# The last pass over the edges also norms and turns its rows for the recurrence

## The chip, the cores and the metric

The kernel runs on one core of one Trainium2 chip, in one launch. The metric is the time of an execution on the device in microseconds (us). The engines of the core are PE (matrix products and transposes), DVE (vector operations), ACT (activations and copies), POOL (vector operations and indirect transfers) and SP (it only issues transfers). ACT and POOL issue transfers too.

## The reference: what is computed

There are N = 3125 nodes with rows x of 256 numbers, and 50000 weighted edges, sorted by their target. Four layers follow each other; each adds its result to x:

1. An attention layer over the edges. Each node's normed row gives features for itself and for its neighbours (128 numbers each, in 4 heads of 32); a node sums its neighbours' features with weights from the edges; both halves are normed by head and added to x.
2. A recurrence over the nodes, taken as one sequence of 3125 steps. With xn the layer norm of the new x, a step computes gates from `xn @ U + b` and from the last state through V: `i`, `o` with a sigmoid, `g` with a tanh, `c = h * c + i * g`, `h = o * tanh(c)`. The states h are added to x.
3. Three graph convolutions (256 to 1024, 512 and 256) with norms.
4. A mixture of eight experts.

The change lies where layer 1 ends and layer 2 begins: the row norm

    xn = (x - mean) / sqrt(var + 1e-5)

of every node, and its transpose, which the products with U read.

## The kernel before, in words

The nodes are padded to 25 tiles of 128 rows. Before the last pass, the edges have been scattered into a dense matrix of weights in DRAM, and that matrix is read back in panels. The sum over the neighbours is a matrix product of features and panels. It runs in 9 passes (`passes`, L581) of 7 steps; a pass takes three row tiles of the matrix (the last one takes one) and a step takes a block of 512 columns, that is four node tiles (the seventh block has one). In a step `products` (L505) issues PE's matmuls, and the count transposes (`ct`, L534) with ACT's Sign (L535), whose result goes to DRAM from two buffers `cs` (L536). The sums lie in `agg0`, two halves of 3200 columns in the pool `ep`, and passes 0 to 7 add to them (L544).

In the last pass the products of a block (L518 and L519, 16 for four tiles) read `agg0` itself and leave the sums, centered and turned, in two banks of PSUM. A bank is one of five (`bank`, L409). A generator, `finish` (L546), ends a block in three stages, which the steps of the pass call one step apart:

- A: the attention weights (L555) and the second half (L558) on DVE, and the square on ACT (L560);
- B: the head's variance on DVE (L563, L564), scale (L565) and power -1/2 (L566) on POOL;
- C: norm (L568) and sum into x (L570) on DVE, and the statistics of each new row of x (L573, L574) into `mv_r`.

So step k holds the products of block k, then A of block k, B of block k-1 and C of block k-2. After the pass come the last B and two C (L957), then the variances are copied (L960) and `inv_sqrt_dve` (L131) takes the inverse root of all 25 tiles into `rstd_r`.

What sets the order: the whole phase stands under `manual_schedule` for DVE, PE, ACT and SP. These four keep the order in which the phase's instructions are written. Instructions written after the phase may be placed among them by the scheduler, and POOL's order is the scheduler's too. A tile whose place in memory belonged to earlier tiles waits until they are free.

Then `recurrence_inputs` (L1050) loads V and U in blocks of 128 columns and six columns of biases, all issued by ACT (L1055, L1068, L1070). For each of 25 tiles it norms the row on DVE (`normalize`, L160), transposes its halves on PE into one of two PSUM tiles (L167) and copies them to `xnT` on ACT (L168). The products with U follow, 42 groups (7 stretches of 500 columns, the last of 125, by 6 gate blocks) of two matmuls (L1083), each evicted by ACT into `xg` with its bias (L1085) from one of four PSUM tiles `pu`.

The recurrence itself (L1154 on) is cut into 125 chains that run side by side for 45 + 25 steps; its first instructions are L1158 on PE and L1180 on ACT. While it runs, POOL gathers the lines for the nodes' degrees (L988), and SP moves them (L1009, L1011). `inv_sqrt` (L124) is the form of the inverse root that runs on POOL (L128, L129).

Of the kernel before, what the change touches and what calls it, by code (L numbers as in the profile page):

```python
# [9 lines left out]
F32 = mybir.dt.float32  # L10
# [3 lines left out]
AF = mybir.ActivationFunctionType  # L14
# [78 lines left out]
def kernel(ctx: ExitStack, tc: tile.TileContext, a: dict, out: bass.AP):  # L93
# [300 lines left out]

    weighed, unit_end = [], []
    ec = ctx.enter_context(tc.tile_pool(name="ec", bufs=1))
    extra_i = ec.tile([P, EXTRA], I32, name="extra_i")
    extra_c = ec.tile([P, EXTRA], F32, name="extra_c")
    line_i = ec.tile([P, NT], I32, name="line_i")
# [2 lines left out]
    with ExitStack() as ph:  # L402
# [21 lines left out]
        nc.gpsimd.memset(zeros, 0.0)  # L424


        agg0 = ep.tile([P, 2, NP], F32, name="agg0")
# [77 lines left out]
        def products(q, j, n, t):  # L505
# [40 lines left out]
            def finish():  # L546

                m0, k = j // P, n // P
                g = k * H0
                f = sp.tile([P, CB // P, 4 * DH], F32, name="fa", bufs=3)  # L550
                fh = f[:, :k].rearrange("p n (h k) -> p (n h) k", k=DH)
                for i in range(0, k, 2):
                    h = min(2, k - i)
                    pt = pas[i // 2].rearrange("p (n o d) -> p n o d", n=2, o=2)[:, :h]
                    nc.vector.tensor_tensor(f[:, i : i + h].rearrange("p n (h k) -> p n h k", k=DH),  # L555
                                            pt[:, :, 0, :].rearrange("p n (h k) -> p n h k", k=DH),
                                            att[:, m0 + i : m0 + i + h, :4, None].to_broadcast([P, h, H0, DH]), ALU.mult)
# [5 lines left out]
                nc.vector.tensor_reduce(var[:, :g], sq[:, :k].rearrange("p n (h k) -> p (n h) k", k=DH), AX.X, ALU.add)  # L563
                nc.vector.tensor_scalar(var[:, :g], var[:, :g], 1.0 / DH, 1e-9, op0=ALU.mult, op1=ALU.add)  # L564
                nc.gpsimd.tensor_tensor(f[:, :k], f[:, :k], sc0[:, None, 4 * DH :].to_broadcast([P, k, 4 * DH]), ALU.mult)  # L565
                nc.gpsimd.tensor_tensor(rs[:, :g], var[:, :g], neghalf[:, :g], ALU.pow)  # L566
                yield
                nc.vector.tensor_tensor(fh, fh, rs[:, :g, None].to_broadcast([P, g, DH]), ALU.mult)  # L568
                xs = x[:, m0 : m0 + k, 4 * DH :]
                nc.vector.tensor_add(xs, xs, f[:, :k])  # L570
                for i in range(m0, m0 + k):
                    st = sp.tile([P, 6], F32, name="st")
                    nc.vector.bn_stats(st, x[:, i, :])  # L573
                    nc.vector.bn_aggr(mv_r[:, i, :], st)  # L574
                yield

            if last:
# [3 lines left out]
        def passes(q, k0=0, k1=7):  # L581

            per = len(steps) // len(PASSES)
            for k in range(q * per + k0, q * per + k1):
                while len(panels) <= k + AHEAD and len(panels) < len(steps):
                    panels.append(load(*steps[len(panels)]))
                now = products(*steps[k], panels[k])
                if rest[0] is not None:
                    rest[0]()
                if q == len(PASSES) - 1:  # L590
                    for g in (now, *ending[-2:][::-1]):
                        next(g)
                    ending.append(now)
                    now = None
                rest[0] = now
# [212 lines left out]
        with ExitStack() as eh:  # L808
# [238 lines left out]

    def recurrence_inputs(rp, stats=None):  # L1050

        blocks = [(g, half) for half in range(2) for g in ("i", "o", "c")]
        V = rp.tile([P, 2, 6 * P], F32, name="V")
        for m, (g, half) in enumerate(blocks):
            nc.scalar.dma_start(V[:, :, m * P : (m + 1) * P],  # L1055
                                a["L0_ffn_V_" + g].rearrange("(c p) n -> p c n", p=P)[:, :, half * P : (half + 1) * P])

        xg = rp.tile([P, 6, CH, QW + NB], F32, name="xg")
        nc.vector.memset(xg[:, :, :, :QW], 0.0)
# [2 lines left out]
        with ExitStack() as eh:  # L1062
            up = eh.enter_context(tc.tile_pool(name="u", bufs=1))
            ps = eh.enter_context(tc.tile_pool(name="up", bufs=2, space=PSUM))
            U = up.tile([P, 2, 6 * P], F32, name="U")
            bias = up.tile([P, 6], F32, name="bias")
            for m, (g, half) in enumerate(blocks):
                nc.scalar.dma_start(U[:, :, m * P : (m + 1) * P],  # L1068
                                    a["L0_ffn_U_" + g].rearrange("(c p) n -> p c n", p=P)[:, :, half * P : (half + 1) * P])
                nc.scalar.dma_start(bias[:, m : m + 1],  # L1070
                                    a["L0_ffn_b_" + g][half * P : (half + 1) * P].rearrange("(p o) -> p o", o=1))
            mv, rstd = stats or x_stats(up)
            xnT = up.tile([P, 2, NP], F32, name="xnT")
            for i in range(NT):
                xn = up.tile([P, D], F32, name="xn", bufs=2)
                normalize(xn, i, mv, rstd)
                transposed(ps, xnT[:, :, i * P : (i + 1) * P], xn, 2)
            for b0 in range(0, NB, 20):
                n = min(20, NB - b0)
                for m in range(6):  # L1080
                    pu = ps.tile([P, 20 * CH], F32, name="pu", bufs=4)
                    for c in range(2):
                        nc.tensor.matmul(pu[:, : n * CH], U[:, c, m * P : (m + 1) * P],  # L1083
                                         xnT[:, c, b0 * CH : (b0 + n) * CH], start=(c == 0), stop=(c == 1))
                    nc.scalar.activation(xg[:, m, :, QW + b0 : QW + b0 + n],  # L1085
                                         pu[:, : n * CH].rearrange("p (b r) -> p r b", r=CH), AF.Identity,
                                         bias=bias[:, m : m + 1])
# [743 lines left out]
```

## Time and profile before

| | |
|---|---|
| runs (us) | 2512.12, 2504.01, 2512.48, 2510.44, 2512.84, 2512.64 |
| median of them | 2512.3 |
| profiled execution, its own time | 2507.33 |
| its span in the profile | 2505.5 |
| mean granted clock of PE | 0.908 |
| PE, DVE, ACT, POOL busy | 82%, 41%, 22%, 30% of the span |
| last pass, first product to last statistics | 640.1 to 688.1 |
| first transpose of a normed row | 691.3 |
| products with U (L1083) | 699.9 to 769.3 |
| first product of the recurrence (L1158) | 771.06 |
| end of the recurrence | about 1105 |

All times within the profile count from the start of its span. The profile is one execution; the median is over others, so a sum made in the profile is carried over as a difference. A line of the timeline gives start, length, engine, line of the program, operation, output and inputs, and the number of like instructions merged; in brackets, how long the engine had been idle and what ended it. A line of the waits gives who waited, for whom, the total in us, how often, and the longest. The granted clock is 1.00 when PE runs at full speed.

### The profile page before, as it was taken

The page shows a single profiled execution, that of the slowest core. Times are in us where ns is not written, and L with a number is a line of the kernel's source. Part 1 is how long each engine was busy: PE and PEld are TensorE (multiplying, and loading weights), DVE is VectorE, ACT ScalarE, POOL GpSimd, SP SyncE. Part 2 cuts the span into 40 slices and gives each one's busy share as a digit, 9 for nine tenths or more (in the row PEclk, how much of TensorE's full clock was granted, in tenths as well). Part 3 has the DMA queues.
Part 4 walks back from the last instruction along what each step waited for, and adds up shares of the span by engine and source line. Part 5 has one row for each costly group of instructions (what it writes and reads, how often), then busy time and mean ns, then how long its engine had stood idle before and what let it go on. Part 6 is the DMA issues. An engine that isn't in the chain of part 4 may idle for free.

```text
span 2505.5 us, 26758 instructions
## 1 busy us (share of the span) xinstructions
PE 2065.2 (82%) x9302; PEld 1436.9 (57%) x9303; DVE 1035.6 (41%) x3090; ACT 543.4 (22%) x1211; POOL 740.2 (30%) x796
## 2 busy tenths in 40 slices
PE   0348679876687699978999999899999988958998
PEld 0224334443445677765566665588888867745665
DVE  3775644556613455574222222111111225443554
ACT  0112212211143233423222222101111201112222
POOL 4677777760405210110111111000000114440111
PEclk9757889888889899988999999999999888878999
DMA  7673577747310000006333322443332286623230
GB/s 258 229 275 118 165 260 257 230 145 252 113 44 25 2 1 1 1 2 229 122 118 122 118 71 82 144 146 114 117 106 80 86 300 217 220 86 102 97 106 19
DMA packets 216671, 324.66 MB, mean 130 GB/s; under 512 B 47053, under 2 KB 114164, under 8 KB 215238
## 3 DMA queue, kind: packets, MB, share of 16 engines
q1 hardware_dynamic: 137312, 242.08, 29.4%
q10 hardware_dynamic: 62646, 73.17, 8.5%
q0 software_dynamic: 16560, 7.53, 1.3%
q8 instruction: 77, 1.26, 0.2%
q14 instruction: 76, 0.62, 0.1%
HBM read 217.52 MB, written 106.97 MB: 130 GB/s over the span
## 4 chain that ended last, share of the span: by engine, by line
PE 32%; issue 12%; POOL 5%; DMA 4%; DVE 1%; ACT 0%; POOLq 0%; ACTq 0%; SPq 0%; DVEq 0%
PE agg L1402 17%; PE pp L1462 6%; PE pz L1514 3%; PE pa L1577 2%; DMA buf<-rw,wr 2%; POOL out_dram L1789 1%; PE agg L1407 1%; DMA w<-in_L_ffn_w_dram 1%; POOL buf L1338 1%; DMA adj<-adj_c 1%; PE phm L1770 1%; POOL y L1607 1%; POOL y L1606 1%; POOL acc L1443 0%; POOL rs L129 0%
## 5 line engine op out<-in xcount | busy, mean ns | idle before, releaser
L382 POOL DMA_INDIRECT adj_w<-sum_w,idx_w x391 | 396.8, 1015 | 158.1 <-issue 115.0
L1402 PE MATMUL agg<-adj,hi 128*128 128x512 f32 (+1 forms) x1050 | 405.0, 392 | 12.5 <-issue 7.1
L1402 PE MATMUL agg<-adj,lo 128*128 128x512 f32 (+1 forms) x1050 | 393.4, 381 | 0.8 <-DMA lo<-lo_d 0.8
L524 PE MATMUL pa<-panel,feat_nei 128*128 128x512 f32 (+1 forms) x672 | 294.5, 590 | 32.3 <-DVE agg L544 30.4
L1443 POOL TENSOR_TENSOR acc<-acc,sq 128x512 f32<-128x512 f32 (+1 forms) x70 | 82.0, 1171 | 609.1 <-issue 488.2
L1402 PEld LDWEIGHTS agg<-adj,hi 128*128 128x128 f32 x1050 | 203.2, 194 | 58.7 <-issue 16.8
L1402 PEld LDWEIGHTS agg<-adj,lo 128*128 128x128 f32 x1050 | 203.3, 194 | 40.9 <-issue 5.2
L1462 PE MATMUL pp<-W,r 128*128 128x512 f32 (+1 forms) x600 | 222.0, 529 | 0.8 <-DVE r L1439 0.8
L524 PEld LDWEIGHTS pa<-panel,feat_nei 128*128 128x128 f32 x672 | 126.3, 205 | 163.2 <-issue 126.3
L1577 PE MATMUL pa<-hl,adj 128*128 128x512 f32 x625 | 170.5, 427 | 8.4 <-DMA adj<-adj_c 7.3
L1462 PEld LDWEIGHTS pp<-W,r 128*128 128x128 f32 x600 | 114.9, 194 | 99.0 <-issue 91.3
L1166 PE MATMUL pg<-hn,V 128*128 128x125 f32 x1104 | 161.1, 279 | 0.0
L535 ACT ACTIVATE cs<-ct 128x768 f32<-128x768 bf16 (+3 forms) x117 | 80.7, 737 | 329.7 <-PE ct L534 299.7
L1577 PEld LDWEIGHTS pa<-hl,adj 128*128 128x128 f32 x625 | 124.9, 205 | 37.2 <-DMA adj<-adj_c 11.6
L1166 PEld LDWEIGHTS pg<-hn,V 128*128 128x128 f32 x1104 | 143.7, 196 | 0.0
L205 PE MATMUL pa<-ident,xn 128*128 128x128 f32 x50 | 15.1, 402 | 138.6 <-DVE xn L160 138.6
L1466 ACT ACTIVATE t<-t,dinv 128x512 f32<-128x512 f32 (+1 forms) x50 | 30.7, 615 | 453.0 <-DVE t L1465 430.1
L544 DVE TENSOR_TENSOR agg<-agg,pa 128x512 f32<-128x512 f32 (+1 forms) x98 | 60.1, 628 | 151.5 <-PE pa L524 151.5
L1158 PE MATMUL pg<-xg,ident 128*128 128x250 f32 x280 | 89.7, 404 | 30.4 <-ACT io L1181 28.5
L1166 PE MATMUL pc<-hn,V 128*128 128x125 f32 x552 | 106.9, 292 | 9.1 <-DVE hn L1185 9.0
L1465 DVE SCALAR_TENSOR_TENSOR t<-pp,rs,bw 128x512 f32<-128x512 f32 (+1 forms) x50 | 30.7, 615 | 200.4 <-PE pp L1462 199.7
L1777 PE MATMUL py<-w,hT 128*128 128x256 f32 (+1 forms) x512 | 113.1, 379 | 0.0
(387 smaller groups left out, 3017.7 us busy)
## 6 DMA issues: line engine op xcount, KB each, us to landing
adj<-adj_c SPq DMA_DIRECT2D x450, 256.0 KB
panel<-adj_w SPq DMA_DIRECT2D x48, 768.0 KB
adj_c<-cs ACTq DMA_DIRECT2D x48, 768.0 KB
w<-in_L_ffn_w_dram ACTq DMA_DIRECT2D x16, 1024.0 KB
adj_w<-zeros SPq DMA_DIRECT2D x4, 3200.0 KB
adj_w<-zeros SPq DMA_DIRECT2D x2, 4800.0 KB
adj_w<-zeros SPq DMA_DIRECT2D x1, 8000.0 KB
adj_w<-zeros SPq DMA_DIRECT2D x1, 6400.0 KB
```

Of the source, the lines that this page charges most:

```text
L382: st = nc.gpsimd.indirect_dma_start(out=adj, out_offset=bass.IndirectOffsetOnAxis(ap=idx[:, t : t + 1], axis=0), in_=val[:, t : t + 1], in ...
L524: nc.tensor.matmul(pa[:, :n], feat_nei[:, c0 + i, o, :], t[:, i, :n], start=(i == 0), stop=(i == k - 1))
L535: nc.scalar.activation(cs[:, i0 : i0 + m, : k * P], ct[:, :m, : k * P], AF.Sign)
L544: nc.vector.tensor_add(to, to, pas[o][:, :n])
L1158: nc.tensor.matmul(pg[u].rearrange("p g b -> p (g b)"), ident, xg[:, 3 * u : 3 * u + 2, r, q : q + NB], start=True, stop=(h is None))
L1166: nc.tensor.matmul(pc[u] if s == 2 else pg[u][:, s, :], V[:, c, m * P : (m + 1) * P], h[:, c, :], start=(c == 0 and s == 2), stop=(c == 1 ...
L1402: nc.tensor.matmul(agg[f][:, :n], part[:, c, f * P : (f + 1) * P], adj[c - g0][:, :n], start=(c == 0 and q == 0), stop=False)
L1443: nc.gpsimd.tensor_add(self.acc2[:, :n], self.acc2[:, :n], sq[:, :n])
L1462: nc.tensor.matmul(pp, self.r[:, o, i * P : (i + 1) * P], self.W[:, o, :], start=(o == 0), stop=(o == self.k - 1))
L1514: nc.tensor.matmul(pz[:, :n], W1[:, f, o * P : (o + 1) * P], s[:, f, :n], start=(f == 0), stop=(f == 1))
L1577: nc.tensor.matmul(pa[i], adj[c - c0][:, i * P : (i + 1) * P], hl[:, c], start=(c == 0), stop=False)
L1777: nc.tensor.matmul(py[:h], hT[:, f, r : r + h], w2[:, f, :], start=(f == 0), stop=(f == 7))
```

## The change

- `agg0` moves from the pool `ep` to a pool of its own on the other side of the memory, which is closed when the inputs of the recurrence are done.
- Stage C also takes the inverse root of its block's variances, with `inv_sqrt` on POOL. A fourth stage, D, is added: DVE forms -mean * rstd (`off_r`), ACT norms each row as an Identity with scale and bias, PE transposes its halves into a bank of the five, two tiles to a bank, and ACT copies a bank to `agg0`, in the columns where the block's sums were.
- Step k of the last pass also runs D of block k-3; after the pass, six calls instead of three finish the last three blocks.
- The variance copy, `inv_sqrt_dve` and the loop of 25 norms, transposes and copies fall away; `recurrence_inputs` gets `agg0` as its `xnT`.
- U, the biases and V are loaded by SP instead of ACT, U ahead of V.

The other call of `recurrence_inputs`, in a branch that runs only for other inputs, keeps its own loop.

The diff, cut to its core:

```diff
+    ag_pool = ExitStack()
+    ag = ag_pool.enter_context(tc.tile_pool(name="ag", bufs=1, side="right"))
+    agg0 = ag.tile([P, 2, NP], F32, name="agg0")
...
+    def input_weights(pool):
+        U = pool.tile([P, 2, 6 * P], F32, name="U")
+        bias = pool.tile([P, 6], F32, name="bias")
+        for m, (g, half) in enumerate(gate_blocks):
+            nc.sync.dma_start(U[:, :, m * P : (m + 1) * P],
+                                a["L0_ffn_U_" + g].rearrange("(c p) n -> p c n", p=P)[:, :, half * P : (half + 1) * P])
+            nc.sync.dma_start(bias[:, m : m + 1],
+                                a["L0_ffn_b_" + g][half * P : (half + 1) * P].rearrange("(p o) -> p o", o=1))
+        return U, bias
...
                     nc.vector.bn_aggr(mv_r[:, i, :], st)
+                blk = slice(m0, m0 + k)
+                inv_sqrt(sp, rstd_r[:, blk], mv_r[:, blk, 1], 1e-5)
+                yield
+
+                off = sp.tile([P, CB // P], F32, name="off_r")
+                nc.vector.scalar_tensor_tensor(off[:, :k], mv_r[:, blk, 0], -1.0, rstd_r[:, blk], op0=ALU.mult, op1=ALU.mult)
+                for i in range(0, k, 2):
+                    h = min(2, k - i)
+                    xn = sp.tile([P, 2, D], F32, name="xn_r")
+                    pt = bank().rearrange("p (c n) -> p c n", c=2)
+                    for o in range(h):
+                        nc.scalar.activation(xn[:, o, :], x[:, m0 + i + o, :], AF.Identity, bias=off[:, i + o : i + o + 1],
+                                             scale=rstd_r[:, m0 + i + o : m0 + i + o + 1])
+                        for c in range(2):
+                            nc.tensor.transpose(pt[:, c, o * P : (o + 1) * P], xn[:, o, c * P : (c + 1) * P], ident)
+                    nc.scalar.copy(agg0[:, :, (m0 + i) * P : (m0 + i + h) * P], pt[:, :, : h * P])
                 yield
...
-                    for g in (now, *ending[-2:][::-1]):
+                    for g in (now, *ending[-3:][::-1]):
                         next(g)
...
-            for g in (ending[-1], ending[-2], ending[-1]):
-                next(g)
-            var = sp.tile([P, NT], F32, name="var")
-            nc.vector.tensor_copy(var, mv_r[:, :, 1])
-            inv_sqrt_dve(sp, rstd_r, var, 1.0, 1e-5)
+            for k in (1, 2, 3, 1, 2, 1):
+                next(ending[-k])
...
+            U, bias = input_weights(up)
             for m, (g, half) in enumerate(blocks):
...
+                nc.sync.dma_start(V[:, :, m * P : (m + 1) * P],
+                                    a["L0_ffn_V_" + g].rearrange("(c p) n -> p c n", p=P)[:, :, half * P : (half + 1) * P])
+            xnT = given
+            if xnT is None:
...
-        V, xg = recurrence_inputs(rp, (mv_r, rstd_r))
+        V, xg = recurrence_inputs(rp, agg0)
+        ag_pool.close()
```

More of the change, by code (lines that the diff above doesn't have):

```diff
@@ L396 @@
     ec = ctx.enter_context(tc.tile_pool(name="ec", bufs=1))
+    ag_pool = ExitStack()
+    ag = ag_pool.enter_context(tc.tile_pool(name="ag", bufs=1, side="right"))
+    agg0 = ag.tile([P, 2, NP], F32, name="agg0")
+    gate_blocks = [(g, half) for half in range(2) for g in ("i", "o", "c")]
+    def input_weights(pool):
[7 more added lines that the diff above has]
+        return U, bias
     extra_i = ec.tile([P, EXTRA], I32, name="extra_i")
@@ L424 @@
         nc.gpsimd.memset(zeros, 0.0)
-        agg0 = ep.tile([P, 2, NP], F32, name="agg0")
         pan = ph.enter_context(tc.tile_pool(name="g0pan", bufs=3))
@@ L1043, in fold, with recurrence_inputs @@
             nc.vector.tensor_scalar_mul(w[:, c, :], w[:, c, :], g[:, c : c + 1])
-    def recurrence_inputs(rp, stats=None):
-        blocks = [(g, half) for half in range(2) for g in ("i", "o", "c")]
+    def recurrence_inputs(rp, given=None):
+        blocks = gate_blocks
         V = rp.tile([P, 2, 6 * P], F32, name="V")
-        for m, (g, half) in enumerate(blocks):
-            nc.scalar.dma_start(V[:, :, m * P : (m + 1) * P],
-                                a["L0_ffn_V_" + g].rearrange("(c p) n -> p c n", p=P)[:, :, half * P : (half + 1) * P])
         xg = rp.tile([P, 6, CH, QW + NB], F32, name="xg")
@@ L1064, in recurrence_inputs @@
             ps = eh.enter_context(tc.tile_pool(name="up", bufs=2, space=PSUM))
-            U = up.tile([P, 2, 6 * P], F32, name="U")
-            bias = up.tile([P, 6], F32, name="bias")
+            U, bias = input_weights(up)
             for m, (g, half) in enumerate(blocks):
[L1068 to L1077, printed above, removed]
+                nc.sync.dma_start(V[:, :, m * P : (m + 1) * P],
+                                    a["L0_ffn_V_" + g].rearrange("(c p) n -> p c n", p=P)[:, :, half * P : (half + 1) * P])
+            xnT = given
+            if xnT is None:
+                mv, rstd = x_stats(up)
+                xnT = up.tile([P, 2, NP], F32, name="xnT")
+                for i in range(NT):
+                    xn = up.tile([P, D], F32, name="xn", bufs=2)
+                    normalize(xn, i, mv, rstd)
+                    transposed(ps, xnT[:, :, i * P : (i + 1) * P], xn, 2)
             for b0 in range(0, NB, 20):
```

## The prediction

> **What bounds the kernel in this stage.** The page comes first. Its row of slices has PE in the nines almost everywhere, but the chain that ended last starts only at 1145 us, so the stage under change (the last pass, 640 to 688 us, and the inputs of the recurrence, to 771 us) has to be read from its own views. I read the waits of 660 to 775 us next.
>
> ```profile
> POOL ln L988 <- ACT xg L1085: 86.4, 1, 86.4
> DVE hc L1153 <- ACT xg L1085: 57.0, 1, 57.0
> PE pt L167 <- DVE xn L160: 24.5, 2, 24.4
> ACT xnT L168 <- DMA U<-in_L_ffn_U_o_dram: 9.0, 1, 9.0
> ```
>
> Every engine waits for the last L1085: the recurrence, one chain of 70 steps, starts when xg is complete (first L1158 at 771.06), and all that follows hangs on it. So whatever moves the end of L1085 moves the end of the kernel one for one. Before that, PE waits 24.4 us for the first normed rows, and ACT 9 us behind the loads of U that it issues itself. Busy time by stretch shows the same hole: in 665 to 690 us PE does one matmul, DVE is full.
>
> ```profile
> 665.00:690.00 25.00, 0.22 (x1) 0.00 (x0) 23.30 (x67) 2.50 (x7) 15.01 (x7) 0.59 0.42 106
> 690.00:700.00 10.00, 2.74 (x11) 1.96 (x12) 2.42 (x9) 1.39 (x4) 0.00 (x0) 0.50 0.78 242
> 715.00:771.00 56.00, 54.48 (x148) 26.02 (x146) 0.00 (x0) 25.36 (x43) 0.00 (x0) 1.00 0.00 0
> ```
>
> (Columns: PE, PEld, DVE, ACT, POOL busy, then granted clock, DMA share, GB/s.) Then the timeline of one step of the last pass on DVE, from one block's first product to the next block's:
>
> ```profile
> 664.15 0.39 DVE L555 TENSOR_TENSOR fa<-pa,att 128x256 f32<-128x256 f32 x1
> ...
> 665.71 0.68 DVE L563 TENSOR_REDUCE fv<-fsq 128x16 f32<-128x512 f32 x1
> ...
> 671.03 0.39 DVE L555 TENSOR_TENSOR fa<-pa,att 128x256 f32<-128x256 f32 x1
> ```
>
> A step takes 6.88 us: 1.56 for the new block (stage A, L555 and L558), 5.32 for B of the block before and C of the one before that. DVE sets this pace because PE ran ahead: its last product is at 664.05, when DVE has only reached the fifth block.
>
> **The change, part by part.** Stage C gains inv_sqrt on POOL; a new stage D of block k-3 stands at the end of step k: one small DVE operation (off), then on ACT two norms, a copy, two norms, a copy, and on PE four transposes ahead of each copy. What decides is order. This phase keeps its written order on each engine, and the waits of PE show that it is kept at a price:
>
> ```profile
> PE pa L928 <- DVE one L926: 10.5, 1, 10.5
> ```
>
> PE stood 10.5 us at one matmul of the extras, with the products of L524 ready behind it. By that order, D's transposes of block k-3 stand on PE ahead of the products of step k+1, and they need ACT's norms, which need off, which is the last DVE instruction of step k. Stage A of step k+1 needs those products. So from the fifth block on PE can't run ahead: DVE, ACT, PE and DVE again wait for each other in a ring, once a step. Queued behind the waiting transposes are the products and the count transposes of step k+1; for them wait DVE's A, ACT's Sign and Square, and then B and C.
>
> Steps 0 to 3 stay as they are (D starts in step 3, the products of steps 0 to 3 are done by about 656): step 3 ends at 664.15 plus off, 0.18 by L564's small row, 664.33. One turn of the ring after that:
> - Two norms on ACT. L1481 (128x256, bias and scale from a tile) ran 23 in 11.42 us, 0.49 each: 1.0.
> - The last two transposes. PE has been idle for over 8 us by then; at what clock do they run? After a gap of 9.85 us at 587.3 these rows stand:
>
> ```profile
> 588.00:590.00 2.00, 0.00 (x0) 0.00 (x0) 1.89 (x7) 1.35 (x2) 0.00 (x0) 1.00 1.06 351
> 590.00:592.00 2.00, 0.00 (x0) 0.00 (x0) 1.89 (x7) 0.16 (x1) 0.00 (x0) 0.75 1.04 311
> ...
> 598.00:600.00 2.00, 2.00 (x4) 0.81 (x3) 1.08 (x2) 0.00 (x0) 0.00 (x0) 0.50 1.05 401
> 600.00:602.00 2.00, 2.00 (x7) 0.80 (x6) 0.00 (x0) 0.00 (x0) 0.00 (x0) 0.69 1.06 406
> ```
>
>  The clock falls to 0.50 some 3.7 us after the last matmul and returns 4.1 us after PE starts again. So I take half clock: four transposes took 1.09 at 691.34, two 0.65 with their end.
> - Copy of 128x512 from PSUM, 0.59 (L542); two more norms 1.0; their transposes 0.65; five handovers of about 0.05. Sum so far 4.15.
> - The products of the first two tiles, 8 matmuls: 20 (16 and 4 count transposes) took 3.85 at full clock, so 1.75, at half clock 3.5. The second eight: 2.1, as the clock returns about 4 us after the first.
> - DVE does the first half of A meanwhile, the second after it, 0.83; then B, C and off, 5.5.
>
> 4.15 + 3.5 + 2.1 + 0.83 + 5.5 = 16.1 us instead of 6.88. The ring's idle time on PE, over 5 us a turn, lets the clock fall each time. Steps 4 and 5 cost 9.2 each; step 6 has one tile, so 4.15 + 1.8 (four matmuls) + 0.55 (A) + 4.7 (B, C, off; 4.48 before from 678.41 to 682.89) = 11.2 instead of 4.98, 6.2 more. DVE reaches the end of its passes at 664.33 + 32.2 + 11.2 = 707.7; before, that point was 682.89. The tail (B, C, C: 5.3 as before) is then covered by ACT, which is the later: D of blocks 3, 4 and 5 at 4.75 each and 1.6 for the last tile give 707.7 + 15.85 = 723.5.
>
> The clock is where the Trainium skill and a row differ. "TensorE: Matmul & The Clock Gate", Part 1 (The HAM clock gate), says that the default is throttled, that an idle window of about 3.4 us halves the clock and that one busy window of that length releases it; by it the second eight matmuls would take 1.75 and a step 15.8. The 0.50 that this trace shows throughout 1108 to 1126 us, with PE busy 1.4 to 1.7 us of every 2, speaks for a later release.
>
> By that row alone a step would stay at half clock, the second eight at 3.5, a step 17.5, the end 2.8 later.
>
> What goes: variance copy and inv_sqrt_dve (688.1 to 690.0), 25 DVE norms and the transposes and copies of 691 to 714.7, with ACT's stop at the loads:
>
> ```profile
> 697.75 0.65 ACT L168 COPY xnT<-pt 128x256 f32<-128x256 f32 x2 [8.97 <-DMA U<-in_L_ffn_U_o_dram]
> 714.66 20.70 PE L1083 MATMUL pu<-xnT,U 128*128 128x500 f32 x49
> ```
>
> At 714.66 six of the 42 groups of L1083 were done; the other 36 (30 of 1.676, 6 of 0.72) ran to 769.3. In the new kernel all 42 are left at 723.5: 36 x 1.676 + 6 x 0.72 = 64.6. If none of them runs earlier they end at 788.1, with 2 for the clock's return 790: 20.8 later than before. The four pu buffers let at most four groups run in PE's gaps while D ends (6.7 and the 2 of the clock): 781.4, 12 later. L1085 itself can't start before, as xg lies where the pass's small tiles lay (an inference from the order of pools; its memset followed the last rstd_r directly before, at 690.80). I take +14, nearer to the lower end: L1083 ran between the transposes before, too (699.92).
>
> Edits that I cost at nothing. The 18 loads on SP, at 0.37 to 0.49 of issue each, 8 us: SP issues nothing between 656 and 816.60 (L1009), so nobody stands behind them, and U is needed only at 712 or later. If its place (by my sum of the pools, the second cs buffer) comes free only with the last adj_c store, it still has some 15 us for 0.75 MB; without that cover it costs what it lands late, 0 to 8. POOL's inv_sqrt: 0.24 and 1.05 (128x4 rows of L128, L129) a block beside 5.0 in a step that grows to 16; it runs in the next step's wait. W1 and W2 and six small loads stay on ACT, about 4 us of issue, and can fall into the ring: 0 to 4. Above 771 nothing changes but the start.
>
> On the loads a page speaks against the change: "DMA: Bandwidth & Descriptors", Issuing engines are not separate DMA queues, says that another issuing engine saves only the sequencer's issue time, as all run on the same 16 engines. By it the move is worth at most the issue time; the wait of 8.97 above, of an ACT copy behind ACT's own loads, is what the trace gives.
>
> **The rivals.**
> 1. Ring, but at full clock. Each pair's transposes 0.35 instead of 0.65, products 1.75 and 1.75: turn 13.4, last step 9.7, end of DVE's passes 700.8, D done 714.6, groups done 772.5 to 779.2: +3 to +10, 2518. For it: the recurrence keeps 1.00 at 91% PE; against it: the rows above.
> 2. No ring: faster. If the order put the products of step k+1 ahead of D's transposes on PE, DVE would keep 6.88 + 0.18; the last C ends at 688.9, its rstd on POOL 1.1 later, D at 692, 64.6 + 2 of groups by 759: -10, 2502. It decides at the fifth block: A at 664.4 instead of 672. Against it: the 10.5 above.
> 3. Worse: the ring at half clock throughout (2.8), ACT's loads inside it (4), U late or no group ahead of D's end (20.8 instead of 12): +20 to +28, 2536. This is also the case in which the new place of the work is right and the loads on SP don't do what they are meant to.
>
> **How the numbers follow.** The profiled execution took 2507.33 us (span 2505.5), the median of the runs is 2512.3, and five of six lie at 2510.4 or above; I add the difference to the median: 2512.3 + 14 = 2526. Chances: forecast (+10 to +20) 0.60, rival 1 0.15, rival 2 0.12, rival 3 0.13. The range takes in the forecast, rival 1 down to no gain and rival 3 but its end: 2512 to 2537; rival 2 and the tails are left out. About 0.2%, 5 us, is what a measurement of this kernel can tell from no change: faster 0.13 (rival 2 and a hundredth), same 0.12 (0.08 of rival 1 and the lower tail of the forecast), slower 0.75.
>
> **What would show it.** Right: L555 of the fifth block starts near 672 instead of 664.15 and waits for PE; steps 4 and 5 take 13 to 17 us; PE's granted clock is near 0.5 from 660 to 725; the first L1158 stands near 785; no wait of ACT for U. Wrong: A of the fifth block still at 664, or L1083 running in numbers before D has ended, which my reading of xg's place excludes.

## The result, and the profile after

| | before | changed |
|---|---|---|
| median of the runs (us) | 2509.93 (2504.01 to 2529.81, 46 runs) | 2532.33 (2526.57 to 2551.83, 20 runs) |
| ratio, 95% interval | | 1.0089 [1.0079, 1.0100] |
| profiled execution, its own time | 2507.33 | 2527.4 |
| its span | 2505.5 | 2525.6 |
| mean granted clock of PE | 0.908 | 0.902 |
| last pass, first product | 640.1 | 639.6 |
| first product of the recurrence | 771.06 | 789.72 |

The kernel became 22 us slower by the medians and 20.1 by the two profiles. 2532.33 lies inside the range on record, 6 us above the predicted time. The forecast was a difference of 14, added to a median of six runs (2512.3); against the median of 46 runs the difference is 22, some 8 us more than that. The stage from the first product of the last pass to the first product of the recurrence, called "the stage" from here on, grew from 130.95 to 150.1 us: nearly all of the difference is there.

The changed program has other line numbers: A is L570 and L573 (before: L555, L558), B L578 to L581, C L583 to L589, `inv_sqrt` L128 and L129, off_r L595; D's norms, transposes and copies are L601, L604, L605; the products of the pass L533 and L534 (L518, L519), the products with U L1107 and their evictions L1109 (L1083, L1085), the recurrence's first products L1183 (L1158).

The waits of the changed kernel between 655 and 800 us, to be held against those of before (who waited, for whom, total, times, longest):

```profile
POOL ln L1016 <- ACT tg L1205: 76.3, 1, 76.3
DVE hc L1178 <- PE pu L1107: 65.6, 1, 65.6
...
PE pa L604 <- ACT xn_r L601: 39.7, 13, 9.3
...
DVE fa L570 <- PE pa L534: 22.9, 5, 7.7
...
ACT xn_r L601 <- DVE off_r L595: 13.7, 3, 4.7
```

The first two rows stand where those of before stood: all still hang on the end of the products with U. The 24.4 us in which PE waited for DVE's norms and the 9 us in which ACT waited for U are gone. In their place stand the three rows of a closed ring: PE waits for ACT, DVE for PE, ACT for DVE.

One turn of it, in the timeline of the changed kernel (PE, DVE and ACT; weight loads left out):

```profile
663.69 0.13 DVE L595 SCALAR_TENSOR_TENSOR off_r<-mv_r,rstd_r 128x4 f32<-128x4 f32 x1
663.86 1.09 ACT L601 ACTIVATE xn_r<-x,off_r,rstd_r 128x256 f32<-128x256 f32 x2 [4.75 <-DVE off_r L595]
...
664.51 1.18 PE L604 MATMUL pa<-ident,xn_r 128*128 128x128 f32 x4 [9.32 <-ACT xn_r L601]
...
666.86 1.18 PE L604 MATMUL pa<-ident,xn_r 128*128 128x128 f32 x4 [1.17 <-ACT xn_r L601]
...
667.83 0.63 PE L533 MATMUL pa<-center,agg 128*128 128x128 f32 x2
...
671.49 0.42 DVE L570 TENSOR_TENSOR fa<-pa,att 128x256 f32<-128x256 f32 x1 [7.67 <-PE pa L534]
...
673.80 0.42 DVE L570 TENSOR_TENSOR fa<-pa,att 128x256 f32<-128x256 f32 x1 [1.43 <-PE pa L534]
...
678.99 1.10 DVE L595 SCALAR_TENSOR_TENSOR off_r<-mv_r,rstd_r 128x4 f32<-128x4 f32 x1
```

Read it downwards: off of block 0 ends at 663.8, ACT norms, PE turns after 9.32 us of standing, the fifth block's products start only behind those transposes, and DVE gets its A after 7.67 us of idling. Then B, C and the next off, and the next turn begins at 680.1. Before, DVE did this A at 664.15.

Busy time by stretch in the changed kernel (PE, PEld, DVE, ACT, POOL, granted clock, DMA share, GB/s):

```profile
665.00:670.00 5.00, 3.83 (x18) 3.22 (x18) 0.00 (x0) 2.16 (x4) 0.59 (x1) 0.50 0.00 0
...
675.00:680.00 5.00, 0.00 (x0) 0.00 (x0) 4.76 (x13) 0.63 (x1) 4.43 (x2) 0.93 0.18 54
680.00:685.00 5.00, 3.05 (x13) 2.25 (x14) 0.09 (x1) 3.25 (x6) 1.30 (x3) 0.50 0.01 3
685.00:690.00 5.00, 4.01 (x33) 3.83 (x32) 1.98 (x5) 0.66 (x2) 0.00 (x0) 0.89 0.00 0
690.00:695.00 5.00, 0.00 (x0) 0.00 (x0) 4.76 (x13) 0.63 (x1) 4.41 (x2) 0.79 0.17 54
...
715.00:720.00 5.00, 2.65 (x11) 1.40 (x10) 0.16 (x1) 3.15 (x6) 0.00 (x0) 0.50 0.25 98
```

DVE and PE take turns: where one is full the other has nothing to do. The clock is 0.50 whenever PE comes back. How D's tail goes over into the products with U, from the timeline of the changed kernel, and the first product of the recurrence:

```profile
722.26 0.37 ACT L605 COPY agg<-pa 128x256 f32<-128x256 f32 x1 [0.78 <-PE pa L604]
...
722.43 0.31 DVE L1084 MEMSET xg<- 128x300 f32 x1 [7.27 <-PE pa L604]
...
722.68 2.03 PE L1107 MATMUL pu<-agg,U 128*128 128x500 f32 x2 [0.46 <-ACT agg L605]
...
789.72 1.51 PE L1183 MATMUL pg<-xg,ident 128*128 128x250 f32 x6 [1.58 <-issue]
```

The first product with U starts 0.05 after the last copy of D: no group ran ahead of it. xg's first writer, the memset, waited for the last transpose.

### The profile page after: what moved, and what is told of

Read it like the earlier page. It is cut to its first block, busy times and chain, and to the rows that moved or that the text cites. A ratio compares the mean times of both kernels' runs of the same rounds, so it can differ in the third digit from the quotient of the medians.

```text
span 2525.6 us, 26727 instructions
## 1 busy us (share of the span) xinstructions
PE 2078.5 (82%) x9302; PEld 1445.3 (57%) x9303; DVE 1025.9 (41%) x3065; ACT 555.8 (22%) x1223; POOL 749.6 (30%) x810
## 4 chain that ended last, share of the span: by engine, by line
PE 32%; issue 11%; POOL 4%; DMA 4%; DVE 1%; ACT 0%; POOLq 0%; DVEq 0%; SPq 0%
PE agg L1427 17%; PE pp L1487 6%; PE pz L1539 3%; PE pa L1602 2%; DMA buf<-rw,wr 2%; POOL out_dram L1814 1%; PE agg L1432 1%; DMA adj<-adj_c 1%; POOL buf L1363 1%; PE phm L1795 1%; POOL y L1632 1%; POOL y L1631 1%; POOL acc L1468 0%; PE pv L1474 0%; POOL rs L129 0%
## 5 line engine op out<-in xcount | busy, mean ns | idle before, releaser
L1427 PEld LDWEIGHTS agg<-adj,hi 128*128 128x128 f32 x1050 | 202.7, 193 | 56.6 <-issue 18.7
L1191 PE MATMUL pg<-hn,V 128*128 128x125 f32 x1104 | 161.1, 279 | 0.0
L1602 PEld LDWEIGHTS pa<-hl,adj 128*128 128x128 f32 x625 | 124.9, 205 | 36.8 <-DMA adj<-adj_c 11.2
L1191 PEld LDWEIGHTS pg<-hn,V 128*128 128x128 f32 x1104 | 143.8, 196 | 0.0
L1191 PE MATMUL pc<-hn,V 128*128 128x125 f32 x552 | 107.1, 292 | 21.7 <-DVE hn L1210 21.7
L1183 PE MATMUL pg<-xg,ident 128*128 128x250 f32 x280 | 90.1, 406 | 32.8 <-ACT io L1206 31.1
```

The costliest lines, as they stand in the source:

```text
L1183: nc.tensor.matmul(pg[u].rearrange("p g b -> p (g b)"), ident, xg[:, 3 * u : 3 * u + 2, r, q : q + NB], start=True, stop=(h is None))
L1191: nc.tensor.matmul(pc[u] if s == 2 else pg[u][:, s, :], V[:, c, m * P : (m + 1) * P], h[:, c, :], start=(c == 0 and s == 2), stop=(c == 1 ...
L1427: nc.tensor.matmul(agg[f][:, :n], part[:, c, f * P : (f + 1) * P], adj[c - g0][:, :n], start=(c == 0 and q == 0), stop=False)
L1602: nc.tensor.matmul(pa[i], adj[c - c0][:, i * P : (i + 1) * P], hl[:, c], start=(c == 0), stop=False)
```

## The experiments

Profiles of single executions, from the kernel before to e8, reach the last pass up to 7 us apart (639.0 to 646.0), so times inside a profile are compared by the length of the stage. Each stage is read from one profile; the change and e8, which differ only in who issues the loads, give 150.1 and 150.2. The ratios are to the kernel before, timed on the same chip. Those of e5, e6 and e8, timed in one batch, give some 3.5 us less than their stages (e8: 15.8 us above before by the ratio, 19.2 by the stage; e7 of the same batch differs by 0.6); their intervals reach 5 to 6 us to either side, so the stage is the finer measure.

| run | ratio, 95% interval | stage (us) |
|---|---|---|
| before | 1 | 130.95 |
| the change | 1.0089 [1.0079, 1.0100] | 150.1 |
| e1_off_early | 1.0027 [1.0017, 1.0037] | 136.3 |
| e2_lag4 | 1.0010 [1.0002, 1.0019] | 129.5 |
| e3_warm | 1.0052 [1.0037, 1.0067] | 143.8 |
| e4_before_sp | 0.9968 [0.9955, 0.9980] | 124.9 |
| e5_split | 1.0028 [1.0007, 1.0049] | 141.7 |
| e6_d_last | 1.0046 [1.0025, 1.0067] | 146.2 |
| e7_lag4_split | 0.9967 [0.9946, 0.9987] | 123.3 |
| e8_loads_act | 1.0063 [1.0039, 1.0087] | 150.2 |
| e9_tail_free | 1.0070 [1.0044, 1.0097] | 150.0 |
| e10_three_ahead | 1.0064 [1.0041, 1.0086] | 145.0 |
| e11_best | 0.9965 [0.9947, 0.9984] | 122.0 |

The theory was the ring, with the half clock inside it. The rivals: the new work is simply too much for some engine, or the loads on SP do harm.

**The ring.** Two edits leave all the work in and change only where one link stands. e1 puts D of block k-3 ahead of C and B on DVE, so that `off` is no longer the last instruction of a step:

```diff
-                    for g in (now, *ending[-3:][::-1]):
+                    for g in (now, *ending[-3:-2], *ending[-2:][::-1]):
```

> Only the place of stage D in a step changes: it is called right after A instead of after C, so the small DVE operation off stands before B and C on DVE. PE's and ACT's orders, the work and the loads stay. Theory (a ring through PE's order: off is the last DVE instruction of a step, and D's transposes stand ahead of the next products): the ring loses B and C, about 5 us a turn. Steps 4 and 5 take 9 to 11 us instead of 15.8 and 15.0, the last block is turned near 707 instead of 722.6, and the time is 13 to 18 us below the changed kernel, some 0.1 to 0.3% above the kernel before. Rival (the added work of ACT, POOL and PE at half clock makes the pass long, wherever off stands): no change against the changed kernel, 0.8 to 0.9% above before.

DVE's first A of blocks 4 and 5 in e1's timeline:

```profile
668.60 0.42 DVE L570 TENSOR_TENSOR fa<-pa,att 128x256 f32<-128x256 f32 x1 [3.28 <-PE pa L534]
...
679.64 0.42 DVE L570 TENSOR_TENSOR fa<-pa,att 128x256 f32<-128x256 f32 x1 [3.51 <-PE pa L534]
```

A turn is 11.0 instead of 15 to 16, since B and C now run while ACT and PE do D; DVE still waits 3.3 to 3.5 for PE. The stage lost 13.8 us of the 19.2 that the change had added, by the place of one small instruction a step. e2 opens the ring: D lags four blocks and is called ahead of A, so its input is ready a step earlier.

```diff
-                    for g in (now, *ending[-3:][::-1]):
+                    if len(ending) > 3:
+                        next(ending[-4])
+                    for g in (now, *ending[-2:][::-1]):
...
-            for k in (1, 2, 3, 1, 2, 1):
+            for k in (4, 1, 2, 3, 1, 2, 1):
```

> D runs one step later (block k-4 in step k), and is called ahead of A, so off is the first DVE instruction of a step and needs nothing of that step. Theory of the ring: it is open, D's transposes are done about 4.2 us into a step and the next products a little after DVE wants them: A of the fifth block near 664, steps of 7 to 8 us; four blocks of D are left for the end, one after the other at 4.7 each, so D ends near 700; 0.05 to 0.2% below the kernel before. Rival (added work and the clock): steps stay above 11 us and the time stays 0.5% or more above before.

The same two rows in e2's timeline:

```profile
664.41 0.42 DVE L570 TENSOR_TENSOR fa<-pa,att 128x256 f32<-128x256 f32 x1
...
672.17 0.42 DVE L570 TENSOR_TENSOR fa<-pa,att 128x256 f32<-128x256 f32 x1 [0.68 <-PE pa L534]
```

The fifth block's A is at 664.41 with no wait, and steps take 7.8 and 8.1. The stage ends 1.4 shorter than before the change. The time doesn't follow: +0.10% where a small gain was expected. Some 2 us are lost again after the stage: from the first product of the recurrence to the product that closes it (`pn`, the test whether the chains agree), e2 takes 337.8, the kernel before 335.7. The rest of the gap, about 2 us, isn't placed.

**The clock.** e3 keeps PE at work while it waits: unused products of zeros ahead of each step's D, in a bank that nobody reads by then. It adds work on PE and leaves the order of all the rest.

```diff
+                    for _ in range((0, 0, 0, 38, 27, 27, 25)[len(ending)]):
+                        nc.tensor.matmul(sums, zero_b[:, :P], zero_b, start=True, stop=True)
                     for g in (now, *ending[-3:][::-1]):
```

> The changed kernel with matrix products of zeros on PE (into a bank that nobody reads any more) between the products of a step and D's transposes, in steps 3 to 6, so that PE's clock stays at full speed; nothing waits for them but PE. Theory (ring, with half clock as a part of its length): PE's granted clock 1.00 in the steps, a turn of about 13.2 instead of 15.0 to 15.8, D's end some 6 us earlier, +0.55 to 0.65% against before instead of +0.89%. Rival 1 (the ring is all, the clock nothing): no change. Rival 2 (the clock is the main cause): the time falls to within 0.2% of before.

In e3's timeline (its pass began 3.4 later than that of the change):

```profile
673.17 0.42 DVE L570 TENSOR_TENSOR fa<-pa,att 128x256 f32<-128x256 f32 x1 [5.55 <-PE pa L534]
...
686.79 0.42 DVE L570 TENSOR_TENSOR fa<-pa,att 128x256 f32<-128x256 f32 x1 [5.54 <-PE pa L534]
```

The turn is 13.6, the stage 6.3 shorter. So the half clock within the turns is a third of the loss (in D's tail, from about 710 on, e3 is back at 0.50); the ring stands without it too. In its turns that is rival 1 of the prediction, which gave 13.4, made real by an edit.

**The order inside D.** e5 lets ACT do all four norms of a block ahead of its two copies, so that ACT doesn't wait for PE between pairs:

```diff
+                turned = []
...
-                    nc.scalar.copy(agg0[:, :, (m0 + i) * P : (m0 + i + h) * P], pt[:, :, : h * P])
+                    turned.append((i, h, pt))
+                for i, h, pt in turned:
+                    nc.scalar.copy(agg0[:, :, (m0 + i) * P : (m0 + i + h) * P], pt[:, :, : h * P])
```

> The changed kernel, but in stage D ACT does all four norms of a block first and its two copies after them. Order of D in the step as in the change, so the ring stays. Theory (ring; its ACT part is norms, copy, norms in a row): the first copy leaves the ring, the way from off to the next products shrinks from 4.15 to 2.75 us, a turn to about 14, and the blocks turned after the pass take 3.2 instead of 4.7 us each; D ends near 714, 8 us earlier than in the changed kernel: +0.5 to 0.6% against before. Rival (DVE's and POOL's work sets the step, ACT's order doesn't): no change, +0.9%.

The stage is 8.4 shorter: the first wait of DVE falls from 7.67 to 6.31, and in the tail a block of D takes 3.3 instead of 4.7.

**D behind the pass.** e6 has the pass of before and all of D after it.

```diff
-                    for g in (now, *ending[-3:][::-1]):
+                    for g in (now, *ending[-2:][::-1]):
...
-            for k in (1, 2, 3, 1, 2, 1):
-                next(ending[-k])
+            for k in (1, 2, 1):
+                next(ending[-k])
+            for g in ending:
+                next(g)
```

> The changed kernel, but all seven D after the pass, none in it. Theory (ring): the pass runs at its old pace (steps of 6.9, C of the last block ends near 688), the whole of D stands behind it, 6 x 4.7 + 1.75 = 30 us one after the other, and ends near 718, only 4 us before the changed kernel's 722.6: +0.7 to 0.75% against before. So the pass would gain by turning nothing within it. Rival (the turns hidden in the pass are worth more than the ring costs): 5 us or more slower than the changed kernel, over +1.05%.

The pass is back at 6.9 a step (661.21, 668.10, 674.98), but twelve pairs of tiles at 2.35 us each and a single tile now follow it, and the products with U start 78.5 after the pass began instead of 83.1. The stage is 3.9 shorter, as the theory had it; the ratio, +0.46%, lies below its 0.7 to 0.75%. To lose the ring alone isn't enough: D has to run beside the pass to be worth anything.

**The loads.** e4 is the kernel before, with nothing changed but that SP issues U, the biases and V, U first. e8 is the changed kernel with these loads back on ACT. The line of e4's edit for U, which e8 turns round:

```diff
-            nc.scalar.dma_start(U[:, :, m * P : (m + 1) * P],
+            nc.sync.dma_start(U[:, :, m * P : (m + 1) * P],
```

> The kernel before with the other part of the change alone: U, the biases and V are loaded by SP, U ahead of V; the last pass and the norms as before. Theory (ACT's copy waited behind ACT's own loads, 8.97 us): the first copies to xnT stand near 692 instead of 697.75, and the kernel is 4 to 6 us faster than before, 0.15 to 0.25%. Rival (U lands when it lands, beside the 3 MB of W1 and W2, whoever issues it): within 2 us of before.

> The changed kernel with U, the biases and V issued by ACT again. Theory (in the changed kernel the ring sets the end, U was there long before): within 3 us of the changed kernel, +0.8 to 1.0% against before, though 18 issues of 0.4 us each stand somewhere among ACT's work. Rival (the loads on SP are worth here what they are worth in e4, some 6 us): +1.1 to 1.2%.

ACT in e4's timeline, at the copies that before had stood 8.97 us behind ACT's loads, until 697.75:

```profile
697.89 0.80 ACT L168 COPY xnT<-pt 128x256 f32<-128x256 f32 x2 [3.25 <-PE pt L167]
...
703.88 0.69 ACT L1085 ACTIVATE xg<-pu,bias 128x500 f32<-128x500 f32 x1 [0.59 <-PE pu L1083]
```

That wait is gone and the stage 6.05 shorter; the whole kernel gains 0.32%. e4 also puts U ahead of V, and no run parts this from the move to SP. In the changed kernel the same edit is worth nothing (150.2 against 150.1), since there ACT's loads run long before anybody needs U. So the change carries one good part, whose gain the rest of it would have covered anyway.

**The two cures together.** e7 is e2 with e5.

> D one step later and ahead of A (as in e2), and ACT's norms ahead of its copies (as in e5). Theory: steps 5 and 6 no longer wait for PE (about 7.1 each), the four blocks left take 3.2 each and end behind the last rstd, near 697 with the pass at 640; from the first product of the pass to the first of the recurrence 124 to 126 us instead of 130.95 before; less 1 to 2 us that the kernels of this family lose at the start of the recurrence: 0.15 to 0.25% faster than before. Rival (the ring was not all: what is left, the tail of D and the late start of the products with U, holds the end): as e2, +0.1%.

In e7's timeline the sixth block's A doesn't wait, and the products with U start 56.9 after the pass began (83.1 in the change, 60 for the first group in the kernel before):

```profile
670.13 0.41 DVE L570 TENSOR_TENSOR fa<-pa,att 128x256 f32<-128x256 f32 x1
```

Its stage is the shortest of these eight, 7.7 below before, and its ratio 0.9967 [0.9946, 0.9987]: faster than both kernels, and by the ratios no better than e4, which moves the loads alone.

**The groups that were to run ahead.** The last three runs were made on a chip on which the kernel before takes 2751.24 us: the part ahead of the last pass is some 240 us longer there (the pass starts at 875 to 881). Stages and ratios are compared, no absolute times. e9 takes D's tail out of the written order and lays pu at the other end of PSUM:

```diff
+            written.close()
             for k in (1, 2, 3, 1, 2, 1):
...
-            ps = eh.enter_context(tc.tile_pool(name="up", bufs=2, space=PSUM))
+            ps = eh.enter_context(tc.tile_pool(name="up", bufs=2, space=PSUM, side="right"))
```

(`written` holds the `manual_schedule` alone.)

> The changed kernel with the calls after the last pass taken out of the written order, and with the PSUM of the products with U (pu) laid at the other end, where it does not meet the banks that D turns into. The step of the forecast that missed is the one that let four groups of products with U run ahead of D's end. Theory A, the written order or the PSUM held them back: some of the first groups stand between D's transposes, the stage (first product of the last pass to the first product of the recurrence) falls from 150.1 by 3 to 6 us, ratio 1.0065 to 1.0075. Theory B, neither did: no group before the last copy of D, stage 150 +- 1, ratio to the kernel before 1.007 to 1.010 as the change itself.

PE in e9's timeline at the end of D:

```profile
955.73 1.18 PE L605 MATMUL pa<-ident,xn_r 128*128 128x128 f32 x4 [0.68 <-ACT xn_r L602]
957.37 8.03 PE L1109 MATMUL pu<-agg,U 128*128 128x500 f32 x13 [0.46 <-ACT agg L606]
```

No group ahead, stage 150.0: theory B. With the tail out of the written order and pu moved, they still stayed behind. No view shows where pu came to lie, so whether all four of its tiles were clear of D's banks isn't known. (D's tail was 4 us shorter here, 11.1 from its first transpose to the first group, and started 4 us later, as the scheduler also put the next block's off and statistics elsewhere.)

e10 puts three groups between the blocks of D by hand, into banks that stay held until xg has its place:

```diff
+            def group_ahead(pu):
+                b = len(ahead) * 20 * CH
+                for c in range(2):
+                    nc.tensor.matmul(pu[:, : 20 * CH], U_e[:, c, :], agg0[:, c, b : b + 20 * CH],
+                                     start=(c == 0), stop=(c == 1))
+                ahead.append(pu)
+
-            for k in (1, 2, 3, 1, 2, 1):
+            for i, k in enumerate((1, 2, 3, 1, 2, 1)):
+                if i == 2:
+                    group_ahead(sums)
+                if i in (3, 5):
+                    group_ahead(bank())
                 next(ending[-k])
```

> The changed kernel with three groups written by hand between D's transposes after the last pass: the first 128 gate columns for the first three stretches of 500 nodes, into banks that stay held until ACT can put them into xg; one sixth of U is loaded for it ahead of the last pass, and loaded again with the rest. The terms on record price a group that runs ahead at 1.68 us. Theory A, PE's gaps in D's tail are free: stage falls from 150.1 by 5.0, to 145, ratio 1.007. Theory B, the tail is the same ring as the steps: a group at half clock (3.35) stands ahead of the next block's transposes and delays them by the part that ACT's two norms (1.0) don't cover, 2.3 for each of two groups, so nothing is left of the 5.0: stage 149 to 151, ratio as the change itself.

PE in e10's timeline (L606 is D's transpose, L994 a group ahead), and the stretch around it:

```profile
950.00 3.07 PE L994 MATMUL sums<-agg,U_e 128*128 128x500 f32 x4
952.91 0.60 PE L606 MATMUL pa<-ident,xn_r 128*128 128x128 f32 x4
954.69 0.93 PE L606 MATMUL pa<-ident,xn_r 128*128 128x128 f32 x4 [1.17 <-ACT xn_r L603]
955.45 1.84 PE L994 MATMUL pa<-agg,U_e 128*128 128x500 f32 x4
...
959.67 1.84 PE L994 MATMUL pa<-agg,U_e 128*128 128x500 f32 x4
961.35 0.38 PE L606 MATMUL pa<-ident,xn_r 128*128 128x128 f32 x2
963.97 6.55 PE L1123 MATMUL pu<-agg,U 128*128 128x500 f32 x15 [2.24 <-ACT xg L1125]
```

```profile
953.00:958.00 5.00, 3.50 (x17) 1.82 (x15) 0.16 (x1) 3.38 (x7) 0.00 (x0) 1.00 0.50 193
```

The stage is 145.0: theory A, to the tenth. The first group runs at half clock (3.07), and by the second the clock is back at 1.00, where the tail of the change stays at 0.50; so the groups pay for their own room, and D ends 83.3 after the pass began, as in the change (83.0). The products left for afterwards take 7.2 less than in the change (three groups, and the clock that needn't return), but start 2.1 later, as ACT first empties the three banks.

That gain is the stage's alone. From the first product of the recurrence to `pn` e10 takes 339.7, the change 336.5 and e9, on the same chip as e10, 336.8: of the 5.0 only 1.9 is left there. No run says why, and the ratio, 1.0064, can't be told from e9's 1.0070.

e11 does the same to e7.

> The version that was best so far (D of block k-4 ahead of the new block's statistics, copies behind all transposes of a block) with the same three groups ahead. Its stage was 123.3, its ratio 0.9967. Theory A: 118.5, ratio 0.995. Theory B: 122.5 to 124, ratio 0.996 to 0.998.

The stage is 122.0, 1.3 below e7's and just under what theory B gave; the ratio, 0.9965 [0.9947, 0.9984], can't be told from e7's. D's tail is as long as in e7, but the next products then wait 3.63 for the banks that the groups hold, and ACT, which must empty them, for its own loads. What ran ahead was mostly given back there, and the rest after the stage (339.0 to `pn`, e7 337.3).

## Why the prediction was right, and where it was off

- **Every engine waits for the last eviction into xg: right.** The stage grew by 19.2, the profiled span by 20.1.
- **The ring from the fifth block on: right.** A of that block was put at 672, it came at 671.49. Turns were put at 16.1; from off to off they took 16.3 (663.8 to 680.1) and 15.0 (680.1 to 695.1). Step 6 was put at 11.2 and took 11.2. DVE's passes were to end at 707.7 and ended at 706.4. e1 and e2 show that it is the ring and not the amount of work.
- **The terms inside a turn.** From off to the first product 4.0 (4.15 on record), the first eight products 3.7 (3.5), the second eight 2.3 (2.1), the second half of A 0.8 (0.83), B, C and off 5.5 (5.5). The first four fit each by itself. The last one fits by luck: off took 1.10 instead of 0.18, and B and C took 4.4 instead of 5.3, since the sum into x took 0.69 instead of 1.63 (the last section shows why). In the second turn the clock came back sooner, and the sixteen products took 4.7 instead of 5.6: that turn was 15.0.
- **Half clock: right.** In the turns it is 6.3 us of the stage (e3). The Trainium skill, "TensorE: Matmul & The Clock Gate", Part 1 (The HAM clock gate), asks for one busy window of about 3.4 us. In the turns the clock came back 4.6 and 2.0 us after the first product (by the granted clock, 0.76 in 670 to 675 and 0.89 in 685 to 690). The tail of the change, PE busy 2.65 of every 5 us with transposes, stays at 0.50 for the 16 us from 707 to 722, while in e10 the clock is back 2.5 us after a group of ordinary products began (0.77 in 952 to 953). The page's Part 4 (PE-mode transpose) says that transposes don't count as busy in the same way. The tail agrees with that, but PE also idled there half the time; and 2.0 and 2.5 us of products are less than that window, unless the transposes right ahead of them counted too. The runs don't part the two causes.
- **D's tail: right.** 4.75 a block was on record, 4.7 measured; it ended at 722.6 (723.5).
- **The loads on SP: right in the sum, wrong in one inference.** They cost nothing (e8). But U's place was free by 624.4, when its loads were issued, and not only with the last adj_c store. In the kernel before, ACT's first copies stood behind the loads that ACT itself issued: of the 8.97 us up to 697.75, 5.9 are the issue of 13 loads and 2.4 a stop between two of them, whose cause isn't shown. So the 6.05 us that e4 gained go well with the rule that another issuing engine saves only issue time ("DMA: Bandwidth & Descriptors", Issuing engines are not separate DMA queues); the page calls that time usually small, and here it was most of the wait, since ACT had copies to do behind it. A load that ACT kept (L1058, issued at 706.20) moved the first norm after the pass by 0.4 (off ended at 706.37, the norm began at 706.76); 0 to 4 was on record for such loads.
- **The step that failed: "I take +14, nearer to the lower end: L1083 ran between the transposes before, too".** The lower end let four groups run ahead of D's end, for 6.7 and the 2 of the clock. None did; 42 groups ran from 722.68 to 788.1, where the text on record had 788.1 for no group ahead and 790 with the clock's return (65.5 us behind D, on record 64.6 and 2). So the recurrence began 18.7 later than before, not 14. The row I leaned on (699.92) was from a kernel in which xg had its place before the first transpose (memset at 690.80); in the changed one the memset, at 722.43, waited for the last transpose, as the text on record expected one sentence earlier. That holds back the evictions. Why the products themselves, which need a bank and not xg, weren't placed earlier isn't settled: e9 changed pu's place and the written order, and they stayed behind; that the scheduler holds them for their evictions is likely and not shown. As for the size of the term, three groups put ahead by hand (e10) took 5.0 off the stage, 1.68 each, but only because two things made up for each other: the clock's return was saved, and ACT's emptying of the banks was added.
- **Not foreseen: about 1 us at the start of the recurrence.** The prediction had "Above 771 nothing changes but the start". From L1183's first product to L1191's it takes 4.6 us, 3.4 before (L1166); up to `pn` 0.8 of it is left (336.5, before 335.7). DVE's timeline of the changed kernel, behind that first product at 789.72:

```profile
791.68 0.31 DVE L1207 TENSOR_TENSOR tg<-tg,io 128x125 f32<-128x125 f32 x1 [1.79 <-ACT io L1206]
792.88 0.34 DVE L1031 TENSOR_SCALAR_CACHE_REDUCE junk_d<-ln,dval 128x125 bf16<-128x125 int32 x1 [0.88 <-DMA ln<-in_dst_dram,line_i]
793.15 0.08 DVE L1031 DVE_READ_ACCUMULATOR junk_d<-ln,dval 128x1 f32 x1
793.15 0.28 DVE L1208 TENSOR_TENSOR cell<-tg,hc 128x125 f32<-128x125 f32 x1
```

  A degree count (L1031) that waits 0.88 us for one of POOL's gathers now stands between two operations of the first step; in the kernel before, the same two followed each other at 773.02 and 773.35, and the first degree count came at 774.83. No run undid this. In e2 and e7 a degree count stands at the same place, and their first steps take 4.2 and 4.5; that is only a part of what they lose after the stage (337.8 and 337.3 to `pn`).
- **The rivals.** Rival 1, the ring at full clock, didn't happen: the clock was 0.50 each time PE came back; e3 shows its turn. Rival 2, no ring, was wrong for this kernel. With the lag made four (e2) the fifth block's A stands at 664.41, as it said, yet the time is 0.10% above before; only with the order of e5 as well (e7) does it come near the gain that it gave (0.33%, 8 us of 10). Rival 3's part "no group ahead" happened, its other parts (loads, half clock throughout) did not. And the whole difference, 20.1 by the profiles and 22 by the ratio, lies in rival 3's band of +20 to +28, just above the forecast's +10 to +20: the ring was right to about a microsecond a turn, and what stood behind it was priced too low.

## What to carry to other kernels

Before work is put into a pipelined loop, write down for each in-order engine which instruction of the next step stands behind the new one, and what the new one waits for. If the last instruction of a step feeds it, and the first instruction of the next step needs what stands behind it, the step's length becomes the sum of all its parts; one more step of lag, or the feeding instruction put first, opens the ring (150.1 to 136.3 and 129.5 us here). And don't count work as running ahead because its inputs are there and because it did so in the old kernel: look at what it and its followers write, and at who has that place until when. Where it matters, write it there by hand, and compare more than the stage (e10 gained 5.0 in the stage and 1.9 up to `pn`).

## What the runs showed of the hardware

A small DVE operation can take as long as the POOL operation beside it. In the changed kernel:

```profile
678.81 1.26 POOL L580 TENSOR_TENSOR fa<-fa,sc 128x512 f32<-128x512 f32 x1
...
678.99 1.10 DVE L595 SCALAR_TENSOR_TENSOR off_r<-mv_r,rstd_r 128x4 f32<-128x4 f32 x1
```

Here off_r ends with POOL's operation, at 680.1; at 663.69 it took 0.13. The Trainium skill, "SBUF — State Buffer", SBUF: two separate sides, has this as one pair of ports that DVE and POOL take as an exclusive lock for a whole instruction. The trace agrees for L580, but not for every operation of POOL: at 663.69, too, POOL was busy, with the power of stage B (L581, 660.92 to 664.27), and beside this power off_r and the sum into x, each with two inputs in SBUF, took no longer than elsewhere. In the ring the stop stands in the critical place, about 1 us at the off of both turns. But it isn't new: before, the same operation of POOL stopped the sum into x instead, which runs free in the changed kernel.

```profile
666.59 1.71 POOL L565 TENSOR_TENSOR fa<-fa,sc 128x512 f32<-128x512 f32 x1 [1.86 <-ACT fsq L560]
667.22 1.63 DVE L570 TENSOR_TENSOR x<-x,fa 128x512 f32<-128x512 f32 x1
...
675.57 3.28 POOL L581 TENSOR_TENSOR fv<-fv,neghalf 128x16 f32<-128x16 f32 x1 [9.98 <-DVE fv L579]
676.12 0.69 DVE L585 TENSOR_TENSOR x<-x,fa 128x512 f32<-128x512 f32 x1
```

(The first two lines are of the kernel before, the last two of the changed one.)
